# A pre-norm attention and expert block: the order of the next operations searched in a queue model while the program is built, projections of all batches in one row

## The chip, the cores and the metric

One core of a Trainium2 chip. A core has TensorE (PE, matrix products into PSUM), VectorE (DVE), ScalarE (ACT), GpSimd (POOL) and SyncE (SP), which issues the transfers between main memory and on-chip memory. PSUM has 8 banks of 128 x 512 fp32. Each engine works through its own queue in order. The metric is device time in microseconds of one launch.

## The reference

x is 4 x 2048 x 256 (four batches, 8192 rows); 16 heads of 16 channels; 8 experts, of which each row takes 2.

```
x = x + attn(layernorm(x))
    attn(x): q, k, v = x @ w_qkv.T + b_qkv
             softmax(q k^T / 16) v per head, @ w_o.T + b_o + x
x = x + ffn(layernorm(x))
    ffn(x): scores = softmax(x @ w_gate.T); the best 2 of 4 groups by the sum of (score + bias), then the best 2 experts
            h = silu(xe @ w1[e]) * (xe @ w3[e]); routed = h @ w2[e]
            out = silu(x @ sw1.T) * (x @ sw3.T) @ sw2.T, and routed rows added to the rows that flat_idx names
```

`flat_idx` holds expert numbers 0 to 7, so that the routed part lands in the first 8 rows of the output only.

## The kernel before, in words

**Attention.** Work is cut into 64 units (batch, group of 4 heads, chunk of 512 queries). For the last batch the units are ordered in two halves of chunks, so that its first chunks end early. A unit has 64 products M (tile mx: 128 queries x 512 keys, with 63 rows contracted), each read by one DVE maximum into ms; the maxima are transposed (mt), negated (mr) and written by a small DMA as row 63 of the unit's queries qst; then 64 products S (tile st: 128 keys x 512 queries), each read by one ACT exponential into et; and 16 steps A (tile av: four matmuls of 128 keys in four column groups), each of which needs four exponentials. At a unit's end ACT copies av to ao and a DMA stores it in ad. M of a unit must be complete before its first S; M runs ahead of S by LEAD (line 32) key tiles beyond a unit. M and S contract 64 rows, alternate between the halves of the array (last digit of the tile's name), and a pair in the two halves runs together.

**Projections and posts.** Each batch has four chunks of projections (`qkv`, line 423: layer norm, transposes pt_x, four qk_proj with tile pp, two v_proj with tile pv, which go to the DRAM tensors kd, qd, vd) and four chunks of posts (`post`, line 845: `heads_in` reads ad and divides by the softmax sums, po is the output projection, then layer norm, transposes, routing (`route`, lgT), and the shared expert pa, pb, pd). `tables` (line 516) multiplies expert weights for the routed part (tile ta). All of these are Python generators that yield what they need next; `step` runs one piece. kd, qd, vd, ad are two DRAM buffers each, used by batch modulo 2; rows 48 to 63 of kd and 16-row padding of qd are written once per buffer from `pad` by `fill_rows` (line 303).

**The order.** PE, DVE, POOL and ACT instructions stand in the order in which the Python program issues them; SP's queue is ordered by the framework. `Plan` (line 36) keeps a clock per engine while the program is built; it decides which pieces are ready, and `mtile` (line 211) takes, of seven banks for M, S and all projections, the one that the plan says is free first. The loop at the end of `body` (line 1345) walks a fixed string:

```
PATTERN = "SADSMMSMDSSPDMMMMSSSASMMSSMAMSSMMSAMMMSS"
```

`token` (line 1303) runs M, S or A, for P a projection block (`do_p`) if its rate says that one is owed, for D a piece of DVE work (`do_d`). The rate spreads what is queued over the batch. `enter` (line 1168) queues, at the first unit of batch b, the projections of batch b+1, the posts of batch b-1 and, in the last batch, the tables. `loads` (line 1186) issues the loads of unit u+2 in unit u, once the projections of its batch are done. When the last A is issued the loop ends; what is left of side jobs, posts and projections is issued after it (`while side or posts or queue`), then the last heads, and `finish` with the last two chunks' shared expert and the routed part (mo, mu, pg).

All instructions go through the wrapper at line 48, so the profile names them L48: they are told apart by tile names, from which numbers of buffers and units are left out.

Of the kernel before, what the change touches and what calls it, by code (L numbers as in the profile page):

```python
# [2 lines left out]

# [25 lines left out]
BIG = 3e38  # L29
LEAD0 = 3  # L30
LEAD = 6
NET = 6
BANKS = 7


class Plan:
# [109 lines left out]

    def book_sp(self, name, out, ins, k):
        self.run("SP", out, ins, 60, self.waits(out, ins, 100), 2300 + out.size() / 40)


def const_array(rows):
# [32 lines left out]
def body(tc, B, L, cols, x, wqkv, bqk, wst, bst, bv, wo, bo, wg, w1, w2, w3, sw1, sw2, sw3, ebias, cst, pad, out):  # L184
# [107 lines left out]

    kst = [cp.tile([P, 2, L], F32R, tag=f"kst{i}", name=f"kst{i}") for i in range(2)]
    qst = [cp.tile([P, 2, QC], F32R, tag=f"qst{i}", name=f"qst{i}") for i in range(3)]
    kd = [dr.tile([H, 64, L], F32, tag=f"kd{i}", name=f"kd{i}") for i in range(2)]
    qd = [dr.tile([H, 64, L], F32, tag=f"qd{i}", name=f"qd{i}") for i in range(2)]
    vd = [dr.tile([P, 4, NK, VW], F32, tag=f"vd{i}", name=f"vd{i}") for i in range(2)]
    ad = [dr.tile([H, 32, L], F32, tag=f"ad{i}", name=f"ad{i}") for i in range(2)]
    resd = dr.tile([B * L, D], F32, tag="resd", name="resd")

    nhalf = cp.tile([P, TQ], F32, tag="nhalf", name="nhalf")
# [56 lines left out]
    def qk_proj(b, c, m, alloc=None):  # L358
        n = f"{b}_{c}_{m}"
        xT = xTs[b, c]  # L360
        w = w_k if m >= 2 else w_q
        tok = slice(c * QC, (c + 1) * QC)
        msl = slice((m % 2) * P, (m % 2 + 1) * P)
        if alloc:
            pp = alloc(f"pp_{n}")
            mm3(pp, w, xT, msl, slice(0, QC))
            yield
        else:
            pp = stile(f"pp_{n}")
            yield from mm3g(pp, w, xT, msl, slice(0, QC))  # L370
        hi = sb.tile([P, QC], F32R, tag="hi", name=f"hi_{n}", bufs=3)
        lo = sb.tile([P, QC], F32R, tag="lo", name=f"lo_{n}", bufs=3)
        f = sb.tile([P, QC], F32, tag="qkf", name=f"qkf_{n}", bufs=2)
        S.activation(f, pp, AF.Identity, bias=b_qk[:, m:m + 1])
        if alloc:
            S.copy(hi, f)
        else:
            S.activation(hi, pp, AF.Identity, bias=b_qk[:, m:m + 1])
        mark["G"] = G.tensor_tensor(lo, f, hi.bitcast(F32), ALU.subtract).ins
        h0 = 8 * (m % 2)  # L380
        dst = (kd if m >= 2 else qd)[b % 2]
        for r, src in enumerate((hi, hi, lo) if m >= 2 else (hi, lo, hi)):
            Q.dma_start(dst[h0:h0 + 8, 16 * r:16 * r + 16, tok], src.bitcast(F32))

    def v_proj(b, c, half, alloc=None):
        n = f"{b}_{c}_{half}"
        xT = xTs[b, c]
        vt = vts[half]
        pv = alloc(f"pv_{n}") if alloc else stile(f"pv_{n}")
        for j in range(2):  # L390
            i = 2 * half + j
            mm3(pv[:, j * D:(j + 1) * D], xT, w_v, slice(i * P, (i + 1) * P), slice(0, D))
            if not alloc and j == 0:
                yield need("c2", 705)
        if alloc:
            yield
        for j in range(2):
            S.copy(vt[:, :, j, 0:68].rearrange("p g (h c) -> p g h c", c=17)[:, :, :, 0:16],
                   pv[:, j * D:(j + 1) * D].rearrange("p (g h c) -> p g h c", g=4, c=16))
        k0 = c * TQ + 2 * half  # L400
        Q.dma_start(vd[b % 2][:, :, k0:k0 + 2, :], vt)

    xls = {}

# [266 lines left out]
    def heads_in(b, c, nh, aT, ahl):  # L671
# [2 lines left out]
        w = H * QC // P  # L674
        s1 = sb.tile([P, w], F32, tag="s1", name=f"s1_{n}", bufs=1)[0:nh * QC // w, :]
        tok = slice(c * QC, (c + 1) * QC)
        Q.dma_start(s1, ad[b % 2][0:nh, 16, tok].rearrange("h (a n) -> h a n", n=w))
        parts = [(t, min(P, 16 * nh - P * t)) for t in range(2) if 16 * nh > P * t]
        for t, np_ in parts:
            Q.dma_start(aT[0:np_, t, :], ad[b % 2][8 * t:8 * t + np_ // 16, 0:16, tok])  # L680
        yield need("d", 480, s1)
        V.reciprocal(s1, s1)
        rd = dr.tile([H * QC], F32, tag="rd", name=f"rd_{n}", bufs=2)
# [198 lines left out]


    queue, posts, side = deque(), deque(), deque()
    todo = [8, 0]
    first_need = need("p")
    wants = {}
# [9 lines left out]

    def load_unit(u):
        b, g, c = units[u]
        for t, src, new in ((qst[u % 3], qd[b % 2][4 * g:4 * g + 4, :, c * QC:(c + 1) * QC], True),  # L900
                            (kst[int(kset[u] % 2)], kd[b % 2][4 * g:4 * g + 4], fresh[u])):
            if new:
                Q.dma_start(t.bitcast(F32), src.rearrange("(p h) r n -> (h r) p n", p=2))

    def load_v(u):
        b, g, c = units[u]
        if fresh[u]:
            vst[kset[u]] = sb.tile([P, NK, VW], F32, tag="vst", name=f"vst_{kset[u]}", bufs=2)
            mark["D"] = Q.dma_start(vst[kset[u]], vd[b % 2][:, g]).ins

    urgent = deque()
    turned = set()
# [42 lines left out]
    def finish_unit(u, av):  # L955
# [4 lines left out]
        def out_():  # L960
            ao = sb.tile([P, QC], F32, tag="ao", name=f"ao_{u}", bufs=1)
            S.copy(ao, av)
            Q.dma_start(ad[b % 2][4 * g:4 * g + 4, :, c * QC:(c + 1) * QC].rearrange("h r n -> (h r) n"), ao)
            if b == B - 1 and g == 3:
                posts.append(post(b, c))
                todo[1] += 12
            if u == len(units) - 2:
                posts.append(post_first(B - 1, NPER - 1))

        urgent.append((need("a", 470, av), out_))  # L970


    ps_p = tc.tile_pool(name="ps_p", bufs=4, space=PSUM)
# [166 lines left out]
    def setup():  # L1140
# [8 lines left out]
            W[n] = split(n, t, eng=G)  # L1149
        with tc.issue_after(mark["D"]):  # L1150
            fill_rows(kd[0], 0, 0, 4)
        for h in (0, 8):
            yield from fill(1, h, h + 8)

    w_g = cp.tile([P, 2, 32], F32, tag="w_g", name="w_g")
    e_b = cp.tile([P, E], F32, tag="e_b", name="e_b")
# [11 lines left out]
    def enter(u):  # L1168

        b, g, c = units[u]  # L1170
        if u == 1:
            posts.append(setup())
        if u % (4 * NPER) == 0:
            for w in range(NPER):
                if b + 1 < B:
                    nqkv[b + 1] = qkv(b + 1, w)
                    queue.append(nqkv[b + 1])
                    todo[0] += 8
                if b:
                    posts.append(post(b - 1, w))  # L1180
                    todo[1] += 12
            if b == B - 1:
                posts.append(tables())
                todo[1] += 9

    def loads():

        u, kt = ns // (4 * NK), ns // 4 % NK
        if u + 2 < len(units) and u + 2 not in loaded and kt >= 4:
            b, g, _ = units[u + 2]  # L1190
            if (nqkv[b] if b else others if g > 1 else None) not in queue:
                load_unit(u + 2)
                loaded.add(u + 2)
        if kt >= NK // 2 and u + 1 < len(units) and u + 1 not in valued:
            load_v(u + 1)
            valued.add(u + 1)
# [6 lines left out]
    def do_s():  # L1203
# [8 lines left out]
            es[ns // 2] = plan.opened("e", NET, sb.tile([P, 2, QC], F32, tag="et", name=f"et_{u}_{kt}_{p}", bufs=NET))  # L1212
        et = es[ns // 2]
        S.activation(et[:, j, :], st, AF.Exp, scale=SCALE)
        ns += 1

    def do_a():
# [8 lines left out]
        for t in e2:  # L1226
            et_free[t.tensor.name] = plan.drained
        na += 1
        if kt == NK - 1:
            finish_unit(u, av)  # L1230

# [11 lines left out]
    def heads():  # L1243

        for n, fn in list(urgent)[:1]:
            yield n, (lambda fn=fn: (urgent.popleft(), fn()))
        for jobs in (side, posts, queue) if todo[1] > todo[0] else (side, queue, posts):
            if jobs:
                yield wants.get(id(jobs[0]), first_need), (lambda jobs=jobs: step(jobs))

# [30 lines left out]
    def do_p():  # L1281

        nonlocal owed
        x = heavy("ms", 150)
        if not x:
            return
        x[1]()
# [2 lines left out]
            lights()  # L1290
            heavy("c", INF)[1]()

    def do_d(most):
        nonlocal credit
        credit = min(1500.0, credit + most)
        while True:
            x = heavy("d")
            if not x or x[0][1] > credit + 300:
                return
            x[1]()  # L1300
            credit -= x[0][1]

    def token(k):
        nonlocal held, owed
        if k == "M":
            if nm < NM and nm // (NK * MXS) in loaded and nm / MXS < ns / 4 + NK + LEAD + 2:
                do_m()
        elif k == "S":
            u = ns // (4 * NK)
            if ns < 4 * NS and ns - 4 * na < 2 * NET:  # L1310
                while u not in turned:
                    if nm < (u + 1) * NK * MXS:
                        do_m()
                    else:
                        urgent_now()
                do_s()
        elif k == "A":
            if held > 0:
                held -= 1
            elif na < NS and 4 * na + 4 <= ns:  # L1320
                do_a()
        elif k == "P":
            left = 4 * NPER * NK - na % (4 * NPER * NK)
            owed = min(3.0, owed + RATE * (sum(todo) + left // NK) / max(8, left // 4 - SPARE))
            for _ in range(2):
                if owed >= 0.5:
                    lights()
                    do_p()
        elif k == "D":
            do_d(450)  # L1330

    def urgent_now():
        while urgent:
            urgent.popleft()[1]()

    PATTERN, LAG, RATE, SPARE = "SADSMMSMDSSPDMMMMSSSASMMSSMAMSSMMSAMMMSS", 2, 1.0, 6
    owed, held, credit = 0.0, LAG, 0.0
    others = rest()
    queue.append(others)
    for h in (4, 8):  # L1340
        for _ in fill(0, h, 2 * h):
            pass
    plan.level()
    with tc.manual_schedule(engines={ENG.PE, ENG.DVE, ENG.Pool}):
        tick = 0
        while na < NS:
            loads()
            lights()
            if nm < NM and nm // (NK * MXS) not in loaded and nm / MXS < ns / 4 + NK + 1:
# [6 lines left out]
                elif light()[1] < INF:  # L1356
                    plan.clock["PE"] = max(plan.clock["PE"], light()[1])
                continue
            token(PATTERN[tick % len(PATTERN)])
            if tick % 8 == 4 and nm / MXS < ns / 4 + NK + LEAD:  # L1360
                token("M")
            tick += 1
        while urgent:
            urgent.popleft()[1]()
    ordered.__exit__(None, None, None)
# [67 lines left out]
```

## Time and profile before

| | |
|---|---|
| median of 3 runs (lowest, highest) | 3239.95 us (3238.51, 3249.52) |
| profiled execution, its own time | 3235.01 us |
| its span, first to last instruction | 3232.6 us |
| mean granted clock of PE | 0.971 |
| busy: PE, weight loads, DVE, ACT, POOL | 3070.5, 1399.5, 2816.2, 2532.3, 540.1 us |
| transfers | 233.81 MB, mean 72 GB/s |

The page's second part shows the same over 40 slices of 81 us (digits are tenths of the slice):

```profile
PE   7899999999999999999999999999999999999968
DVE  7799989998899998997899999999789899899456
ACT  5688878887878788888688888888687777777834
PEclk9899999999999999999999999999999999999978
```

and its fifth part the groups of instructions (engine, operation, out<-in, shapes, count, then busy us, mean ns of one, and the engine's idle time before them):

```profile
L48 DVE TENSOR_REDUCE ms<-mx 128x1 f32<-128x512 f32 x4096 | 2526.4, 682 | 238.8 <-PE mx L48 194.7
L48 ACT ACTIVATE et<-st 128x512 f32<-128x512 f32 x4096 | 2153.6, 604 | 497.3 <-PE st L48 377.5
L48 PE MATMUL st<-qst,kst 64*128 64x512 f32 x4096 | 1245.6, 439 | 62.4 <-DMA qst<-mr 26.2
L48 PE MATMUL mx<-kst,qst 63*128 63x512 f32 x4048 | 1197.3, 452 | 20.6 <-DVE ms L48 8.3
L48 PE MATMUL av<-et,vst 128*32 128x512 f32 x8192 | 1116.3, 617 | 16.4 <-ACT ao L48 16.1
```

Successive instructions of an engine overlap, so the mean of one is longer than the distance from one to the next; a step A appears as eight matmuls.

### The profile page before, as it was taken

Reading aid. Unit: us, or ns where it says so; the run is one execution under the profiler, and the core shown is the slowest. Engines: PE = TensorE matmul, PEld = TensorE weight load, DVE = VectorE, ACT = ScalarE, POOL = GpSimd, SP = SyncE. Lnnn points to the kernel's source line nnn. Section 1 sums busy time; section 2 is a strip of 40 time slices with the busy share of each in tenths; the row PEclk is TensorE's granted clock in tenths of the full one; section 3 lists DMA queues with packets and bytes.
Section 4 is the critical chain, followed back from the end, with each engine's and each line's share of the span. In section 5 each row is a group of like instructions: output and inputs, shape, how many; then the busy total and the mean of one; then the engine's idle time right before and its main releaser. Section 6 shows DMA issues by size and latency. Waiting matters only on the chain. (4 is left out here: it accounts for less than half of the span.)

```text
span 3232.6 us, 52783 instructions
## 1 busy us (share of the span) xinstructions
PE 3070.5 (95%) x19507; PEld 1399.5 (43%) x19507; DVE 2816.2 (87%) x5053; ACT 2532.3 (78%) x4979; POOL 540.1 (17%) x498
## 2 busy tenths in 40 slices
PE   7899999999999999999999999999999999999968
PEld 5434444443444444444344444444344344444346
DVE  7799989998899998997899999999789899899456
ACT  5688878887878788888688888888687777777834
POOL 5101011010112112211111112121011111110143
PEclk9899999999999999999999999999999999999978
DMA  5543131131212122222112122222112111212010
GB/s 155 181 144 100 49 105 50 44 104 33 79 46 98 48 87 67 80 82 67 59 37 93 56 64 93 74 69 65 58 47 76 62 66 68 75 34 79 25 47 27
DMA packets 135677, 233.81 MB, mean 72 GB/s; under 512 B 13179, under 2 KB 70651, under 8 KB 130427
## 3 DMA queue, kind: packets, MB, share of 16 engines
q1 hardware_dynamic: 135419, 230.44, 21.6%
q8 instruction: 153, 2.51, 0.3%
q14 instruction: 105, 0.86, 0.1%
HBM read 134.87 MB, written 103.41 MB: 74 GB/s over the span
## 5 line engine op out<-in xcount | busy, mean ns | idle before, releaser
L48 DVE TENSOR_REDUCE ms<-mx 128x1 f32<-128x512 f32 x4096 | 2526.4, 682 | 238.8 <-PE mx L48 194.7
L48 ACT ACTIVATE et<-st 128x512 f32<-128x512 f32 x4096 | 2153.6, 604 | 497.3 <-PE st L48 377.5
L48 PE MATMUL st<-qst,kst 64*128 64x512 f32 x4096 | 1245.6, 439 | 62.4 <-DMA qst<-mr 26.2
L48 PE MATMUL mx<-kst,qst 63*128 63x512 f32 x4048 | 1197.3, 452 | 20.6 <-DVE ms L48 8.3
L48 PE MATMUL av<-et,vst 128*32 128x512 f32 x8192 | 1116.3, 617 | 16.4 <-ACT ao L48 16.1
L48 PEld LDWEIGHTS st<-qst,kst 64*128 64x128 f32 x4096 | 610.0, 188 | 670.1 <-DVE ms L48 412.2
L48 PEld LDWEIGHTS mx<-kst,qst 63*128 63x128 f32 x4048 | 559.1, 188 | 603.8 <-DVE ms L48 352.8
L48 PEld LDWEIGHTS av<-et,vst 128*32 128x32 f32 x8192 | 162.9, 108 | 348.1 <-issue 308.7
L48 POOL TENSOR_TENSOR lo<-qkf,hi 128x512 fp32r<-128x512 f32 x64 | 81.9, 1282 | 590.9 <-ACT hi L48 439.9
L48 POOL TENSOR_TENSOR rs_a<-rs_a,nhalf 128x4 f32<-128x4 f32 x16 | 16.3, 1019 | 424.1 <-DVE rs_a L48 404.5
L48 POOL TENSOR_TENSOR aT<-aT,rb 128x512 f32<-128x512 f32 x30 | 38.7, 1293 | 274.8 <-DMA rb<-rd 273.4
L48 POOL TENSOR_TENSOR th<-th,cs 128x512 f32<-128x512 f32 x30 | 31.2, 1041 | 302.6 <-ACT th L48 302.6
L48 POOL TENSOR_TENSOR hT<-hT,th 128x512 f32<-128x512 f32 x30 | 38.9, 1297 | 251.2 <-ACT hT L48 113.2
L48 DVE TENSOR_TENSOR x<-pd,x 128x512 f32<-128x512 f32 x32 | 22.1, 690 | 64.1 <-PE pd L48 64.1
L48 ACT ACTIVATE qkf<-pp,b_qk 128x512 f32<-128x512 f32 x64 | 44.3, 692 | 36.7 <-PE pp L48 36.5
L48 POOL TENSOR_TENSOR rs_b<-rs_b,nhalf 128x4 f32<-128x4 f32 x16 | 16.2, 1015 | 284.6 <-DVE rs_b L48 264.1
L48 ACT ACTIVATE x<-x,rs_b 128x256 f32<-128x256 f32 x64 | 33.1, 589 | 18.2 <-DVE rs_b L48 18.2
L48 POOL TENSOR_TENSOR x<-x,xl 128x256 f32<-128x256 f32 x64 | 46.5, 757 | 0.0
L48 DVE TENSOR_TENSOR x<-po,res 128x512 f32<-128x512 f32 x32 | 22.1, 691 | 27.3 <-PE po L48 27.3
L48 POOL TENSOR_TENSOR x<-x,b_o 128x256 f32<-128x256 f32 x64 | 45.4, 743 | 0.0
L48 ACT ACTIVATE xl<-x,rs_a 128x256 f32<-128x256 f32 x64 | 33.2, 590 | 10.3 <-DVE rs_a L48 10.3
L48 ACT COPY ao<-av 128x512 f32<-128x512 f32 x63 | 38.9, 617 | 0.2 <-PE av L48 0.2
(397 smaller groups left out, 2190.8 us busy)
## 6 DMA issues: line engine op xcount, KB each, us to landing
kst<-kd SPq DMA_DIRECT2D x19, 2048.0 KB
qst<-qd SPq DMA_DIRECT2D x63, 512.0 KB
qd<-hi SPq DMA_DIRECT2D x64, 256.0 KB
kd<-hi SPq DMA_DIRECT2D x64, 256.0 KB
ad<-ao SPq DMA_DIRECT2D x63, 256.0 KB
vst<-vd SPq DMA_DIRECT2D x20, 664.0 KB
vd<-vt SPq DMA_DIRECT2D x32, 332.0 KB
x<-x SPq DMA_DIRECT2D x16, 512.0 KB
```

The source lines that it names most:

```text
L48: r = f(*a, **k)
```

## The change

The fixed string, `token` and `do_d` go. A class `Ahead` holds a queue model of PE, DVE and ACT with seven banks, the exponentials' buffers and the accumulator, in nanoseconds. Each turn of the loop fills a window of 46 letters (M, S, A, O for the copy of av, P, D), orders it so that it can run, searches it with 1600 random moves or swaps that are accepted by cost and a falling temperature, and issues the first 10. The window is then filled again. The projections of batches 1 to 3 are all queued at the start, and `rate` spreads projections and posts over all units, with a due time of 2.5 units before a batch begins; a batch's post is queued when the chunk's last group of heads ends. The DRAM tensors kd, qd, vd, ad become four each, and `setup` fills the padding of batches 1 to 3 at once. `loads` takes the next unit when it is closer than two units, too.

```diff
+HORIZON = 46
+COMMIT = 10
+TURNS = 1600
...
+class Ahead:
...
+    def run(self, seq, i, state):
+        (pe, g0, g1, drained, f0, f1, mode, dve, act, ban, exps, free, nm, ns, na, no, vfree, ip, idd) = state
...
+        for c in seq[i:] if i else seq:
+            if c == "M" or c == "S":
...
+                w = ban[0] + 55
+                slow = 0
+                if w > x - 100:
+                    slow = 100
+                    if w > x:
+                        x = w
...
+                pe = x + 4
+                x += 395 + slow
...
+                if c == "M":
+                    x += 40
+                    if x > dve:
+                        dve = x
+                    dve += 598
+                    heapreplace(ban, dve + 85)
+                    nm += 1
+                else:
...
+                    act += 468
+                    heapreplace(ban, act + 105)
+                    exps.append(act + 160)
+                    ns += 1
+            elif c == "A":
+                if len(exps) < 4 or (na % 16 == 0 and no < na // 16):
+                    return None
...
+                pe = g0 = g1 = x + 907
...
+        cost = max(pe, dve - 1500, act - 1500)
+        return cost + 0.3 * (max(pe - dve, 0) + max(pe - act, 0))
...
+    def search(self, seq, state, turns):
...
+        for _ in range(turns):
+            new = seq[:]
+            a = int(rnd() * n)
+            b = int(rnd() * n) if rnd() < 0.5 else a + int(rnd() * 13) - 6
...
+            if rnd() < 0.5:
+                new.insert(b, new.pop(a))
+            else:
+                new[a], new[b] = new[b], new[a]
...
+            cost = self.run(new[i * step:], 0, marks[i])
+            temp *= 1 - 4.0 / turns
+            if cost is None or (cost > now and rnd() > exp((now - cost) / temp)):
+                continue
...
+        return best
...
-    kd = [dr.tile([H, 64, L], F32, tag=f"kd{i}", name=f"kd{i}") for i in range(2)]
+    kd = [dr.tile([H, 64, L], F32, tag=f"kd{i}", name=f"kd{i}") for i in range(B)]
...
-            if b == B - 1 and g == 3:
+            if g == 3:
                 posts.append(post(b, c))
                 todo[1] += 12
+                posted.append((b, c))
...
-        urgent.append((need("a", 470, av), out_))
+        copies.append(out_)
...
-        for h in (0, 8):
-            yield from fill(1, h, h + 8)
+        for i in range(1, B):
+            for h in (0, 8):
+                yield from fill(i, h, h + 8)
...
-        if u % (4 * NPER) == 0:
-            for w in range(NPER):
-                if b + 1 < B:
-                    nqkv[b + 1] = qkv(b + 1, w)
-                    queue.append(nqkv[b + 1])
-                    todo[0] += 8
-                if b:
-                    posts.append(post(b - 1, w))
-                    todo[1] += 12
-            if b == B - 1:
-                posts.append(tables())
-                todo[1] += 9
+        if u == 4 * NPER * (B - 1) + 1:
+            posts.append(tables())
+            todo[1] += 9
...
+    def rate():
+        done = made / NK
+        r = (sum(todo) + 12 * max(0, nchunk - 2 - len(posted)) + len(units) - done) / max(0.5, len(units) - SPARE - done)
+        return max(r / NK, due())
+
+    def due():
+        done = made / NK
+        return max([(todo[0] - 32 * (B - 1 - b) + 16 * b - SOON - done) / max(1.0, 16 * b - SOON - done)
+                    for b in range(1, B) if nqkv[b] in queue], default=0.0) / NK
...
+    LAG, SOON, SPARE = 2, 2.5, 1.5
...
+    for b in range(1, B):
+        for w in range(NPER):
+            nqkv[b] = qkv(b, w)
+            queue.append(nqkv[b])
+            todo[0] += 8
...
-            token(PATTERN[tick % len(PATTERN)])
-            if tick % 8 == 4 and nm / MXS < ns / 4 + NK + LEAD:
-                token("M")
-            tick += 1
+            state = refill()
+            window, rest_ = search.ordered(window, state)
...
+            window = search.search(window, state, TURNS)
+            for c in window[:COMMIT]:
+                if c == "M" and (nm >= NM or nm // (NK * MXS) not in loaded):
+                    continue
+                give(c)
+                lights()
+            window = window[COMMIT:] + rest_
```

`present` reads the model's start from the plan's clocks, and the next blocks and DVE pieces from the heads of the queues; `refill` tops the window up to 46 letters, four S, up to five M and one A at a time (an O after a unit's last A), puts a P in for each block that the rate says is owed, and a D for each ready piece of DVE work; `give` issues one letter.

## The prediction

> **What bounds the kernel now.** I cut the span at four events (first S 96 us, last row-maximum 3027, last A 3081, end) and read the busy time of each stretch; then, inside the long stretch, the waits; then the places where PE or DVE stood longest; then SP's queue there; then the tail.
>
> Stretches (columns: from:to, length, busy us and instructions of PE, weight loads, DVE, ACT, POOL, then granted clock, DMA share, GB/s):
>
> ```profile
> 0.00:96.00 96.00, 73.34 (x321) 52.39 (x323) 71.65 (x136) 50.04 (x94) 49.80 (x59) 0.96 0.53 166
> 96.00:3027.00 2931.00, 2836.60 (x18091) 1244.26 (x18088) 2640.83 (x4697) 2375.24 (x4651) 415.93 (x378) 0.98 0.22 72
> 3027.00:3081.00 54.00, 52.82 (x334) 19.85 (x330) 9.27 (x32) 49.79 (x100) 13.52 (x10) 1.00 0.11 38
> 3081.00:3232.60 151.60, 107.77 (x769) 83.03 (x767) 94.41 (x189) 57.19 (x136) 60.88 (x53) 0.79 0.12 37
> ```
>
> Call them start, main, close, tail: 96 + 2931 + 54 + 151.6 = 3232.6. In main no engine is full: DVE 90%, ACT 81%, and PE's 97% needs a second look. The skill's rule ("Perfetto Trace Analysis", Identifying the Most-Contended Engine) says that matmul busy time is no measure of PE's headroom and that the weight-load share is; that is 1244/2931 = 42%. By PE's busy row a new order could give 3%; by the rule, PE would be half free. I take neither, but add PE's work up from starts in the timeline:
>
> ```profile
> 1095.88 0.18 PEld L48 LDWEIGHTS mx<-kst,qst 63*128 63x128 f32 x1 [0.84 <-ACT et L48]
> ...
> 1096.82 1.07 PE L48 MATMUL av<-et,vst 128*32 128x512 f32 x8
> 1097.82 0.29 PEld L48 LDWEIGHTS mx<-kst,qst 63*128 63x128 f32 x3 [0.84 <-DVE ms L48]
> ...
> 1098.72 1.06 PE L48 MATMUL av<-et,vst 128*32 128x512 f32 x8
> ```
>
> An A holds PE 1.00 us (1096.82 to 1097.82); six S and M, three in each half of the array, 0.90 (to 1098.72): 0.235 a pair plus 0.19 for the turn. Six 512-column matmuls of a projection start to start take 1.5. Over main's built order that is 999 A x 0.907 = 906, pairs 998, turns 360, projections and transposes 303: PE sums to 2567 us, 88%. DVE: long runs of row-maxima stand 0.598 apart (12.65 us for 21), so 4020 of them are 2410, plus 180 of layer norms, additions and routing: 2590, 88%. Two engines are equally loaded, and each waits for the other through seven PSUM banks.
>
> How coarse that coupling is: I cut main at every A and add up, per piece, the longest of the PE, DVE and ACT sums (ACT 0.48 per exponential). One-A pieces give 2861, two-A pieces 2805, four-A pieces 2724. Main took 2931, of which some 40 are the stops below; 2891 is the one-A sum and 1%. So today hardly anything is evened out between one A and the next. **This is what a better order can win.**
>
> The stops:
>
> ```profile
> 776.64 0.38 SPq L48 DMA_DIRECT2D qst<-qd  x1
> 777.70 1.33 SPq L48 DMA_DIRECT2D qst<-mr  x2
> ```
> ```profile
> 780.37 0.47 PE L48 MATMUL st<-qst,kst 64*128 64x512 f32 x1 [3.55 <-DMA qst<-mr]
> 1578.67 0.76 PE L48 MATMUL st<-qst,kst 64*128 64x512 f32 x1 [4.01 <-DMA qst<-mr]
> ```
> ```profile
> 1519.36 0.69 DVE L48 TENSOR_TENSOR x<-pd,x 128x512 f32<-128x512 f32 x1 [10.80 <-PE pd L48]
> ```
>
> Six times the first S of a unit waits for its row of negated maxima, because on SP a load of qst that must wait for the unit before to end stands ahead of it; DVE then idles 5.0 to 5.6. Twice (ends of batches 1 and 2) DVE idles 10.8 + 2.1: 24 S run without an M, as the next batch's queries are not projected yet.
>
> **The change, part by part.**
>
> *Searched order.* Counts in main stay (4,019 M, 1,006 A). Turns hardly change (q stretches 1,242 to 1,283 over the loop; A still come singly but for six pairs). What changes is the mix: 3 M or 7 M per A before, 1 to 8 after, and M and S take turns. The same ledger on the new order: one-A pieces 2830, two-A 2728, four-A 2680. Lower end for main without stops: the four-A sum, if seven banks even out that far; upper end: the one-A sum plus the same 1%, 2858. The planner's prices agree with rows (M 598 ns against 0.598, A 907 plus a drain against 1.00, exponential 468 against 0.478 at best), so I take the nearer row for a planned order: two-A plus 1%, **2755**. Against it: 327 A now stand at most four S behind the ones they need (before: two), so a late exponential reaches PE.
>
> *Projections in one row.* The 24-S droughts at units 30 and 46 are gone from the order; they are in the ledger already. The counterpart is that loads no longer alias two DRAM buffers; DRAM waits were not on any path.
>
> *SP's queue.* Every load and row write counts: in the built order six qst loads again stand ahead of a row write they should follow (units 2, 3, 11, 24, 41, 58 for 8, 14, 15, 16, 32, 48). No gain, 32 + 8 stay.
>
> *Padding of four buffers.* New: eight writes of 16 rows x 8 heads x 2048 x 4 B = 1.05 MB, in one block with the two that existed, ahead of unit 3's query load. Before, the last of those is issued at 162.5 and that load at 163.3. 8.4 MB at 261 to 322 GB/s (100:110 and 190:200 of the windows) is 26 to 32 us that SP's queue is late. Unit 3's first M is the 192nd, 116 after the 76 of the start, at 0.73 each: about 181. The load lands near 197, PE stands with S and A queued behind that M. Range 0 (there is slack I can't see) to 35 (the row of unit 2, behind a 2 MB key load, is later still); I take **18**. Main: 2755 + 40 + 18 = 2813, or 118 less.
>
> *Close.* Before, 91 S, 25 A and four projection blocks followed the last M. After, 64 S and 18 A and no block, but the last four M stand behind 14 S, so the row of the last unit is not ready: 0.2 for the last maximum, 0.9 transpose, copy and hand-overs, 2.7 from the row's issue to the S (777.70 to 780.37 above), then 64 exponentials x 0.534 = 34.2 (the 8.62 us of sixteen at 3026.13) and the last A with its copy, 3: **41**, 13 less.
>
> *Tail.* The cost that the edit does not show. The loop ends before its posts are done: by the built order, 96 pd, 48 pa, 48 pb, 72 po beyond (3,2) and (3,3), and all 32 table matmuls follow the last A, where before 24, 12, 12 and 18 and no table did. That is chunk (2,2) from its transposes, (2,3), (3,0), (3,1), one behind the other. Before's tail shows one chunk alone:
>
> ```profile
> 3078.95 0.39 PE L48 MATMUL po<-w_oh,at_1h 128*128 128x256 f32 x1
> ...
> 3087.87 2.16 PE L48 MATMUL pt_x<-cs,x 128*128 128x128 f32 x8 [4.01 <-ACT x L48]
> ...
> 3113.07 0.39 PE L48 MATMUL po<-w_oh,at_2h 128*128 128x256 f32 x1 [0.59 <-ACT at_2h L48]
> ```
>
> 34.1 us from one po to the next, 25.2 from the transposes. After: 25.2 + 3 x 34.1 = 127.5, and 7 for the tables (eight weight loads over two buffers that the tanh tiles share; 0 to 20). Before, 31.6 lay behind the last A. So **+103**, tail 254. Inside the loop a chunk is 12.9 us of PE. The clock rule ("TensorE: Matmul & The Clock Gate", HAM oscillation) speaks against the move too: PE's idle gaps beyond some 3.4 us halve the clock. Here the gap before pd was 5.6 and pd matmuls then stand 0.21 apart, against 0.12 for po at full clock; the tail's clock is 0.79. At full clock 24 of them would take 2.8 instead of 5.1, a chunk some 31; the row, slow clock included, is what I use.
>
> **Sum.** 96 + 2813 + 41 + 254 = 3204 span, 28 below 3232.6. The profiled execution took 3235.0, 2.4 more than its span, and lies 5 below the median of 3240: 3207 against it, **3212** on the median's scale, 0.9% faster. A measurement of this kernel can tell 0.5% from nothing.
>
> **Rivals.**
> 1. *The leftover chunks decide: slower.* The order stays close to the one-A row: 2858 + 58 = 2916, sum 3307, 3315 on the median's scale; with half the gain, 3264. The point is main's saving: tail and close cost 103 - 13 = 90, so main, padding included, must fall below 2841. For it: the new order still has 697 q stretches of six, like 706 before, and PE and DVE at 88% each leave little. Against: planner prices match the rows. Chance 0.38, about 3270.
> 2. *The two cancel*: main, padding included, saves 74 to 106: 3224 to 3256. Chance 0.16.
> 3. *The banks even out four A's, the padding is hidden*: 2680 + 27 + 40 = 2747, sum 3138 + 8 = 3146. For it: lead of M over S is steady at 84 to 94, so the search can shift work. Against: one bank holds one tile, and S, M and projections share seven. Chance 0.13.
> 4. *The order does nothing because DMA paces main*: its share there is 0.22; dropped.
>
> **How the numbers follow.** Forecast 3165 to 3224, 0.33; rival 3, 0.13; cancelling 0.16; rival 1, 0.38. Faster 0.46, same 0.16, slower 0.38. The range reaches from rival 3 almost to rival 1's upper sum, **3146 to 3310**, and leaves about 0.07 and 0.1 outside; the forecast's own is 3165 to 3224.
>
> **What would show it.** Main from first S to last row-maximum near 2813, with DVE idle down from 290 to about 200 and no 10.8 us gap; a stop of PE near 180 to 200 us with DMA above 0.8; about 41 us from the last maximum to the last A; a tail near 254 with four po blocks 34 apart and the clock below 0.8. Wrong if main saves less than 90 with the padding, if chunks in the tail overlap (tail under 220), or if PE waits for et before av by more than a few tens of us.

## The result: a little slower, and the profile after

| | before | after |
|---|---|---|
| median (lowest to highest), 5 runs each | 3239.7 us (3238.5 to 3249.5) | 3263.5 us (3260.1 to 3267.7) |
| ratio, 95% interval | | 1.0070 [1.0051, 1.0089] |
| span of the profiled execution | 3232.6 us | 3258.3 us |
| mean granted clock of PE | 0.971 | 0.960 |

The time was forecast at 3212 us, faster; it is 24 us (0.7%) slower than before. The slices of 81 us:

```profile
PE   7849999999999999999999998999999999998668
DVE  7748999898999989999999998989999998993456
PEclk9879999999999999999999999999999999999678
```

Three things stand out against before. The third slice of PE and of DVE has a hole (4). The middle of DVE's row has more nines. The last four slices thin out, and the clock with them (6, 7, 8), where before only two did. The same in the windows of the trace, cut at the same four events (columns as in the prediction):

```profile
0.00:96.00 96.00, 73.33 (x320) 51.94 (x322) 72.30 (x137) 49.81 (x93) 49.80 (x59) 0.96 0.52 163
96.00:2958.80 2862.80, 2767.15 (x17875) 1195.20 (x17873) 2608.99 (x4611) 2338.15 (x4609) 375.73 (x343) 0.98 0.22 74
2958.80:2998.50 39.70, 36.85 (x214) 11.87 (x215) 2.71 (x10) 34.26 (x70) 1.02 (x1) 0.91 0.08 24
2998.50:3258.30 259.80, 182.06 (x1101) 143.64 (x1101) 144.63 (x296) 87.44 (x207) 115.56 (x95) 0.73 0.16 50
```

Main fell by 68, close by 14, tail rose by 108: together the 26 us of the spans. The counts matter: main has 86 DVE instructions fewer than before (4,611 for 4,697), the tail 107 more. Work was moved out of main, so part of the 68 is no better order at all.

The groups of instructions, with DVE's and PE's idle time before them:

```profile
L54 DVE TENSOR_REDUCE ms<-mx 128x1 f32<-128x512 f32 x4096 | 2525.7, 680 | 246.3 <-PE mx L54 186.3
L54 PE MATMUL mx<-kst,qst 63*128 63x512 f32 x4048 | 1252.5, 445 | 58.5 <-DMA qst<-qd 40.5
L54 PE MATMUL st<-qst,kst 64*128 64x512 f32 x4096 | 1249.4, 442 | 33.8 <-DMA qst<-mr 19.7
```

A new wait of M for a load of queries, 40.5 us, has come; the wait of S for its row has fallen from 26.2 to 19.7. In the timeline the 40.5 is a single stop, and SP's queue ahead of it shows why:

```profile
224.73 0.76 PE L54 MATMUL mx<-kst,qst 63*128 63x512 f32 x1 [40.53 <-DMA qst<-qd]
```
```profile
170.79 0.63 SPq L54 DMA_DIRECT2D qd<-pad  x1
175.37 0.63 SPq L54 DMA_DIRECT2D kd<-pad  x1
180.19 0.63 SPq L54 DMA_DIRECT2D qd<-pad  x1
185.06 5.40 SPq L54 DMA_DIRECT2D kd<-hi  x2
194.74 0.58 SPq L54 DMA_DIRECT2D kd<-lo  x1
199.57 0.37 SPq L54 DMA_DIRECT2D qst<-qd  x1
```

Before, the same load was issued at

```profile
163.31 0.51 SPq L48 DMA_DIRECT2D qst<-qd  x1
```

The padding's first writes, up to the one at 170.79, are issued 0.67 us apart, the later ones 4.6 to 4.9. A write is 1.05 MB, and 1.05 MB in 4.8 us is 219 GB/s; all transfers between 170 and 200 us moved 212 GB/s. So the queue seems to take a new write only as fast as an old one is done. Unit 3's load is issued at 199.57, 36 us later than before, and it is there only 25 us after that, when M starts.

For what follows I divide main again, in all kernels alike: *stops*, which are the idle gaps of DVE of 3 us or more in the timeline, and *order*, which is the rest. Before: 57 and 2874. After: 86 (40.2 of them the stop at 225 us) and 2776.

### The profile page after: what moved, and what is told of

The parts are those of the page before. It is cut to its first block, busy times and chain, and to the rows that moved or that the text cites. A ratio compares the mean times of both kernels' runs of the same rounds, so it can differ in the third digit from the quotient of the medians.

```text
span 3258.3 us, 52647 instructions
## 1 busy us (share of the span) xinstructions
PE 3059.4 (94%) x19507; PEld 1402.7 (43%) x19507; DVE 2828.6 (87%) x5053; ACT 2509.7 (77%) x4979; POOL 542.1 (17%) x498
## 5 line engine op out<-in xcount | busy, mean ns | idle before, releaser
L54 PE MATMUL mx<-kst,qst 63*128 63x512 f32 x4048 | 1252.5, 445 | 58.5 <-DMA qst<-qd 40.5
L54 PE MATMUL st<-qst,kst 64*128 64x512 f32 x4096 | 1249.4, 442 | 33.8 <-DMA qst<-mr 19.7
L54 PE MATMUL av<-et,vst 128*32 128x512 f32 x8192 | 1103.7, 609 | 7.2 <-ACT et L54 6.7
L54 PEld LDWEIGHTS mx<-kst,qst 63*128 63x128 f32 x4048 | 589.2, 186 | 625.5 <-DVE ms L54 274.1
L54 PEld LDWEIGHTS st<-qst,kst 64*128 64x128 f32 x4096 | 592.6, 186 | 617.5 <-DVE ms L54 304.9
L54 ACT ACTIVATE hi<-pp,b_qk 128x512 fp32r<-128x512 f32 x56 | 38.2, 682 | 4.2 <-DMA qd<-hi 4.2
```

The source lines that it names most:

```text
L54: r = f(*a, **k)
```

## The experiments

All ratios stand against the kernel before on the same chip, where its median was 3248 to 3249 us. When the changed kernel was measured it was 3240 us, so single times and parts compare across kernels only to some 10 us. "M", "S", "A", "P" and "D" are the letters of the window, and a chunk has 24 pd matmuls.

**The padding alone, taken out of the change and put into the kernel before.** e1:

```diff
-        for i in range(1, B):
-            for h in (0, 8):
-                yield from fill(i, h, h + 8)
+        for h in (0, 8):
+            yield from fill(1, h, h + 8)
...
             posts.append(setup())
+        if u in (4, 6, 8, 10):
+            posts.append(fill(2 + (u > 6), 8 * (u // 2 % 2), 8 * (u // 2 % 2) + 8))
```

> The searched kernel, with the padding of batches 2 and 3 written in four lots of two at units 4, 6, 8 and 10 instead of eight writes in one block at unit 1. Theory P (the block holds up unit 3's query load): the one stop of PE of 40.5 us near 184 to 225 us goes, the first 300 us of main lose about 40, time near 3263 - 40 = 3223; the tail stays near 260. Rival: the load is late for another reason (the 0.5 MB loads of x around it, or the projections it reads), the stop stays above 20 us and the time at 3250 or more.

Measured 3222.7 us, ratio 0.9916 [0.9891, 0.9940]: theory P. e3 is the kernel before with four DRAM buffers of each kind and all of `fill(1..3)` in `setup`:

> The kernel before with four DRAM buffers of each kind and the padding of all of them in one block, its order untouched. Theory P: a stop of about 40 us at unit 3's first M, time 3240 + 40 = 3280. The prediction's size: 18, so 3258. Rival (the stop needs the new order's other loads): below 3245.

Measured 3282.3, ratio 1.0102 [1.0079, 1.0125], with a stop of 37.0 us of M for qst<-qd at 216: theory P again, in the old order. And e6, with batch 2's padding at the start and batch 3's in two lots later:

> The changed kernel with the padding of batch 2 still at the start, that of batch 3 in two lots at units 8 and 10: four extra writes in the block instead of eight. Theory (each of the writes holds up unit 3's query load by its own transfer): the stop of 40.5 us shrinks by four times 4.8 us, the distance between SP's issues there, to 21; time about 3243. Rival A (the stop begins only past some depth of the queue): under 8 us, about 3225. Rival B (it is the wait of that load behind others, not the padding's amount): over 33, about 3257.

Measured 3246.6 in a single execution, so without an interval. M in the pages of e1, e6 and e3:

```profile
L54 PE MATMUL mx<-kst,qst 63*128 63x512 f32 x4048 | 1255.3, 446 | 20.0 <-ACT et L54 6.8
L54 PE MATMUL mx<-kst,qst 63*128 63x512 f32 x4048 | 1255.1, 445 | 38.4 <-DMA qst<-qd 20.8
L48 PE MATMUL mx<-kst,qst 63*128 63x512 f32 x4048 | 1202.1, 453 | 56.8 <-DMA qst<-qd 37.0
```

So 0, 4 and 8 extra writes (e1, e6, after) give stops of 0, 20.8 and 40.5 us on PE: 5 us for each 1.05 MB, and no slack shows. The order part is 2776 in after, 2777 in e1 and 2780 in e6, so the padding touches little else.

**No search** (e2):

```diff
-TURNS = 1600
+TURNS = 0
```

> The searched kernel with no search turns: the window is issued as it is filled and made runnable (S, M, A in turn, a P at place 12, a D at place 4). Theory L (the search pushes P and D letters behind the ten that are issued, and so leaves four chunks and the tables behind the last A): by the built order nothing is left behind but the last two chunks, the tail falls from 260 to about 120. Theory O (the search packs main better): main rises from 2862 to 2960 or more, as M, S and A in plain order leave the banks empty or full. Both together: near 3230. Rival to O (the search packs nothing): main within 40 of 2862 plus 40 for the chunks that come into it, and a time near 3165.

Measured 3418.1, ratio 1.0516 [1.0494, 1.0538]. Theory L's tail came (114), and main rose by 296 us, where theory O said 100 or more. The refill's order without moves is far worse than the string of before: its order part is 3104, 230 above before's. Page of e2, the groups of row-maxima and of M:

```profile
L54 DVE TENSOR_REDUCE ms<-mx 128x1 f32<-128x512 f32 x4096 | 2539.2, 681 | 399.8 <-PE mx L54 372.8
L54 PE MATMUL mx<-kst,qst 63*128 63x512 f32 x4048 | 1158.1, 449 | 98.3 <-DVE ms L54 57.9
```

DVE waits for PE 373 us where in after it waits 186, and M waits for banks that DVE still reads (57.9 us): each waits for the other. To learn whether the runs of four S and five M were to blame, I laid both down in turns, with no search and the padding spread (e7), and then two and two (e9; the diff is e7's):

```diff
-            more += ["M"] * max(0, min(want, 5))
+            m = max(0, min(want, 5))
+            more = [c for k in range(5) for c in "MS" if k < (m if c == "M" else len(more))]
```

> No search (TURNS = 0), but the refill lays M and S down in turns (M S M S ... A) instead of four S, then up to five M, then A; padding spread as in e1. In e2 the unsearched order stood 125 us above the sum over one-A pieces, where before, after and e4 stood within 70 below to 13 above it. Theory (runs of one kind use up the banks, and PE, DVE and ACT take turns in standing still): alternation alone brings main back to about the order before: total 3150 to 3210. Rival (it is the search over all letters that packs; alternation is not enough): e2 less the padding's 40, 3340 or more; in between, both.

> As e7, no search and the padding spread, but the refill lays M and S down two and two (M M S S ... A). M and S of the same number use the same half of the array, so e7's single turns put 3858 M and S right behind one of the same half, which alone is 190 us by 0.235 each; two and two put 23 so. Theory (the mix decides, e7 failed for the halves alone): 3160 to 3230. Rival (a fixed mix, with P and D put in between, isn't enough; the search finds where each P, D and M goes): e2 less the padding's 40: 3330 to 3390.

Measured 3416.3 and 3390.9, ratios 1.0519 [1.0494, 1.0545] and 1.0450 [1.0423, 1.0477]: the rival's numbers, twice, but not its reason. How M and S are mixed is not what counts, and the ledger does not see the loss: its one-A sums of 2984, 3002 and 2989 for e2, e7 and e9 lie within 2% of the 2946 of the searched e5 below. M and S of the same half behind one another, which I priced at 190 us, cost at most the 26 us between e7's main and e9's; in the trace PE starts both as two M, two S, two M, two S.

What the three unsearched orders have in common is the place of A. All three refills lay four S and mostly four M between one A and the next. Cut PE's row from the first S to the last M into runs of M and S that nothing else interrupts. The runs sum to 1757 us in e9 and 1786 in e7 against 1502 in e5, for 8,018 to 8,048 products; all else on PE adds up to 1371 to 1386. In e9 717 of the runs have eight products and take 1.71 us (median); in e5 670 have six and take 0.91, and its 48 runs of eight take 1.70. Here is one of eight in e9 (PE's rows, and of the weight loads, PEld, the last) and one of six in e5:

```profile
1504.70 0.50 PE L54 MATMUL mx<-kst,qst 63*128 63x512 f32 x2
1505.04 0.40 PE L54 MATMUL st<-qst,kst 64*128 64x512 f32 x2
1505.28 0.40 PE L54 MATMUL mx<-kst,qst 63*128 63x512 f32 x2
1505.52 0.96 PE L54 MATMUL st<-qst,kst 64*128 64x512 f32 x2
1505.98 0.18 PEld L54 LDWEIGHTS st<-qst,kst 64*128 64x128 f32 x1 [0.51 <-DVE ms L54]
1506.40 1.07 PE L54 MATMUL av<-et,vst 128*32 128x512 f32 x8
```
```profile
1508.19 0.50 PE L54 MATMUL mx<-kst,qst 63*128 63x512 f32 x2
1508.52 0.40 PE L54 MATMUL st<-qst,kst 64*128 64x512 f32 x2
1508.77 0.40 PE L54 MATMUL mx<-kst,qst 63*128 63x512 f32 x1
1508.77 0.39 PE L54 MATMUL st<-qst,kst 64*128 64x512 f32 x1
1509.09 1.07 PE L54 MATMUL av<-et,vst 128*32 128x512 f32 x8
```

The eighth product's weights wait 0.51 us for DVE to finish a maximum. Seven banks serve M, S and projections, so waiting for a bank is the likely reading. The fixed string of before has 705 runs of six and 430 of seven, and at like work its order part lies within some 20 to 30 us of the searched ones (worked out below), not 235 to 273 above. So most of the packing does not take a search. That the length of the runs is the cause rests on these traces; no run changes it alone.

**Pieces P and D kept where the refill puts them** (e4; the search moves M, S, A and O only):

```diff
-            if not 0 <= b < n or new[a] == new[b]:
+            if not 0 <= b < n or new[a] == new[b] or new[a] in "PD" or new[b] in "PD":
```

> The searched kernel in which the search may not move the letters P and D, so that they come up when they were put in; all else as it is, padding in one block. Theory L: nothing but the last two chunks is left behind the last A, tail near 120 instead of 260; main takes three and a half chunks and the tables back, 13 us of PE each: 2862 + 45 to 60 = 2910 to 2920; time near 3175 (3150 to 3200). Rival: what the search wins it wins by choosing where projection blocks stand; then main goes to 2980 or more and the time to 3240 or more.

Measured 3177.0, ratio 0.9776 [0.9753, 0.9798]: theory L. By the built order 48 pd are left behind the last A instead of 144, and no table; the tail is 114. The padding is still paid, in another place. Its block is issued behind the load of queries this time, the last write at 197.7, but ahead of a row of unit 2, on which an S waits until 34 us after the row's issue:

```profile
202.77 5.72 SPq L54 DMA_DIRECT2D qst<-mr  x2
```
```profile
237.24 0.76 PE L54 MATMUL st<-qst,kst 64*128 64x512 f32 x1 [29.80 <-DMA qst<-mr]
```

**Both repairs together** (e5: e4's edit and e1's), and **only D fixed** (e8: e1's edit, and the search may move P):

> P and D pieces keep the places of the refill (as in e4) and the padding of batches 2 and 3 is written in four lots between units 4 and 10 (as in e1). In e4 the eight writes still cost a stop, only in another place: the first S of unit 2 waited 29.8 us for its row. Theory (leftover and padding are two prices that add): that stop goes, e4's 3177 less some 30: 3139 to 3155, with a tail of 114 as in e4. Rival (the writes must be paid somewhere; four at a time they stand before a row write or a load that PE needs): 3170 or more.

> Padding spread; only D is kept where the refill puts it, P may be moved. By the built order 36 more pd and 36 more po stay behind the last A than in e5. Theory (the price is the number of chunks left, each some 36 us in the tail and some 19 to 20 inside main): 20 to 30 above e5, tail 160 to 175. Rival (what moving P wins in main pays for the chunks left): equal to e5 or below.

e5 took 3139.9, ratio 0.9671 [0.9642, 0.9699]: **3.3% faster than before**, the best of all. e8 took 3185.3, ratio 0.9808 [0.9784, 0.9832]. The windows of e5 and of e8, main and tail:

```profile
96.00:2984.70 2888.70, 2847.72 (x18301) 1247.93 (x18298) 2660.18 (x4763) 2383.05 (x4701) 444.60 (x397) 0.99 0.23 77
3024.30:3137.80 113.50, 84.03 (x669) 65.45 (x664) 72.37 (x145) 47.12 (x117) 42.32 (x38) 0.85 0.10 31
```
```profile
96.00:2984.80 2888.80, 2822.62 (x18178) 1228.52 (x18178) 2646.96 (x4723) 2369.88 (x4680) 424.52 (x384) 0.99 0.23 76
3026.30:3183.00 156.70, 111.41 (x793) 86.12 (x785) 95.20 (x190) 58.29 (x138) 63.05 (x54) 0.79 0.12 39
```

Main is equally long in both, though e8 has 40 DVE instructions fewer in it; they reappear in a tail longer by 43. So e8 is 45 above e5, more than the 20 to 30 expected: of what the lighter main saves (order 2846 for 2869), stops take back all (43 for 20, among them eleven waits for a row, 25.9 us).

**P and D laid down earlier** (e10: e5 with places 4 + 8 p and 2 + 6 d):

> e5 with P laid down at places 4 + 8 p of the window instead of 12 + 16 p, and D at 2 + 6 d instead of 4 + 12 d. By the built order only one po block fewer is left behind the last A, the other leftovers are equal. Theory (what is left sets the tail, and main holds the same work): within 12 of e5's 3140, tail 110 to 114. Rival (pieces issued sooner than their inputs make DVE and PE wait in order): 3155 or more, with stops of DVE behind transfers or projections.

Measured 3159.8, ratio 0.9739 [0.9712, 0.9767]. A miss for both: the tail is 109, near what was expected, but main is some 20 us longer than e5's, and not by stops (16 us): the order itself packs worse. It has 557 runs of six where e5 has 670.

The parts of all kernels (us; the start is 96 in each; leftover is pd matmuls behind the last A in the built order):

| | order | stops | close | tail | span | leftover |
|---|---|---|---|---|---|---|
| before | 2874 | 57 | 54 | 152 | 3233 | 72 |
| after | 2776 | 86 | 40 | 260 | 3258 | 144 |
| e1 padding spread | 2777 | 50 | 41 | 259 | 3222 | 144 |
| e6 half of the padding early | 2780 | 69 | 41 | 259 | 3245 | 144 |
| e3 before with padding | 2882 | 94 | 54 | 152 | 3277 | 72 |
| e2 no search | 3104 | 54 | 46 | 114 | 3413 | 48 |
| e7 in turns, no search | 3142 | 16 | 47 | 114 | 3415 | 48 |
| e9 in pairs, no search | 3121 | 11 | 46 | 115 | 3389 | 48 |
| e4 P, D fixed | 2871 | 58 | 40 | 114 | 3179 | 48 |
| e8 D fixed, spread | 2846 | 43 | 42 | 157 | 3183 | 84 |
| e5 P, D fixed, spread | 2869 | 20 | 40 | 114 | 3138 | 48 |
| e10 the same, earlier | 2893 | 16 | 41 | 109 | 3154 | 48 |

e3 has the same M, S and projections between its A as before, and e6 the same as after; their orders differ by 9 and 4 us all the same. Differences of that size in this column say nothing. Of e2's stops, 43 us are one wait of DVE for a load of x near 231; with the padding spread (e7) that wait is 5.

## Why the forecast went to the wrong side

Against the sum of 3204 for the span, 3258.3 came: 54 more. Two terms of the sum failed, both in main: the padding was taken at 18 us and cost 40, and the searched order was taken at 2755 and took 2776. These 43 us alone turn the 28 forecast as a gain into a loss. By steps:

- **Padding, "I take 18": wrong, 40.2.** +22. M was due at 181 and stopped at 184. The landing of the load was forecast near 197, which is about when it was issued (199.6): I took the issue for the landing, which came 25 us later, and then let "there is slack I can't see" stand for a reason. e6 and e1 show none. The rate was too high as well: 261 to 322 GB/s, read in two stretches of the kernel before, where the block ran at some 212 to 219. It came out even above the range's 35.
- **Searched order, "two-A plus 1%, 2755": 2776.** +21. It lies midway between the new order's one-A and two-A sums (2830 and 2728): by that measure the search evens out less than two A's. And of the gain of 98 against before's 2874, about half or more is not packing: the forecast said that the counts stay, and looked at M and A only, while three chunks of posts and the tables had left main, which the ledger booked as gain. What they are worth there can be estimated from e5 against e8 and e1, all with the padding spread: order falls by 23 for 36 pd (1.5 chunks) and by 92 for 96 pd (4 chunks and tables), 15 to 23 a chunk, where the forecast spoke of 12.9. (The letters that the search may move differ between these runs too, so the price holds both.) Three chunks are 45 to 69 of the 98. e8, with nearly before's leftover (84 pd for 72), is 28 below before in order and 40 in order and close together, half a chunk included: at like work its search packs some 20 to 30 us better than the string.
- **Stops, "32 + 8 stay": 46 without the padding.** +6, but by other causes than forecast. The two droughts of 10.8 are gone, as said, and S's waits for rows fell over the whole span from 26.2 to 19.7. New ones came, the largest a wait of 9.5 for M at 1965, and this one:

```profile
743.96 0.55 DVE L54 RECIPROCAL s<-s 128x64 f32<-128x64 f32 x1 [7.89 <-DMA s<-ad]
```

  Here DVE stands in order behind a transfer for a post. That wait for s in main is 7.9 to 8.5 us in after, e1 and e6, where D may move, and nowhere over 2 in e4, e5, e8 and e10, where it may not.
- **Close, 41: right, 39.7.**
- **Tail, 254: right, 259.8.** The first po of the leftover chunks, one of each:

```profile
3020.86 0.39 PE L54 MATMUL po<-w_oh,at_3h 128*128 128x256 f32 x1 [0.55 <-ACT at_3h L54]
...
3056.93 0.39 PE L54 MATMUL po<-w_oh,at_0h 128*128 128x256 f32 x1 [0.32 <-ACT bT L54]
...
3095.04 0.58 PE L54 MATMUL pd<-s_2h,hT_0h 128*128 128x256 f32 x1 [10.28 <-ACT hT_0h L54]
...
3102.66 0.38 PE L54 MATMUL po<-w_oh,at_1h 128*128 128x256 f32 x1 [0.55 <-ACT at_1h L54]
...
3137.03 0.38 PE L54 MATMUL po<-w_oh,at_2h 128*128 128x256 f32 x1 [0.55 <-ACT at_2h L54]
```

  They stand 36.1, 45.7 and 34.4 apart (forecast 34.1, and 7 for the tables); the longest holds a wait of 10.28 for ACT. The clock of the tail fell from 0.79 to 0.73, the direction in which the rule on the clock gate that the prediction cites pointed. The price of a chunk was read from a row at the slow clock, so most of it was in the sum already.
- **Late exponentials before A** (tens of us, if wrong): 6.7 us in all. Didn't come.

Sum: 22 + 21 + 6 - 1 + 6 = 54. **Rival 1's outcome is what happened**, and its point held: tail and close cost 94 (forecast 90), main had to fall below 2841, and it was 2863. Its premise did not hold: the order did not stay at the one-A row of 2858 but fell to 2776, and the padding took back the difference to its form "with half the gain, 3264". That 3263.5 was measured, so close to it, is luck. With the padding spread main is 2827 and the kernel is faster than before. Repairing the other half, the leftover, pays more: 1.5 chunks cost 43 in the tail, 4 chunks 146, which is 29 to 36 a chunk for 15 to 23 inside. In spans the two repairs give 36 and 80 alone and 121 together, so they add up, nearly.

What e5 wins over before, 95 us of span, comes from order 5, stops 37, close 14 and tail 38. Order and close belong together, since main took in work from both: it has 210 PE instructions more than before, close 113 fewer (221 for 334) and the tail 100 fewer. In the stops the two droughts are gone, and the waits for a row fell from 26.2 to 2.2 us. So "this is what a better order can win", as the forecast put it, named the smaller part: most is in stops and at the end.

Open: why the search puts P and D off past the letters that are issued, beyond the fact that forbidding it brings the leftover from 144 pd to 48; why hardly an S waits for its row in e5; and whether runs of six would pack as well without any search in the new kernel.

## What to carry to other kernels

Before booking a lower sum for a stretch as better packing, count in the built order what has left the stretch, and price it where it went: here a chunk cost some 15 to 23 us inside and 29 to 36 behind the end. A sum of work per piece doesn't see who waits for whose bank inside the piece: look at how long runs of a given length take before trusting it. A scheduler that issues only the head of its window needs a rule against putting off side work. Where a block of large writes is moved ahead of a load, take the whole queue time, landing included, and no discount for slack that no row shows; then spread the block.

## What the hardware showed unexpectedly

- Writes of 1.05 MB each are issued 0.67 us apart at first and then 4.6 to 4.9 (after); each one more ahead of the load made PE stop 5 us longer (0, 20.8, 40.5 for 0, 4, 8).
- The same block, issued after that load instead (e4), stopped an S for 29.8 us at its row of 4 KB: here a small transfer was as late as the large ones ahead of it in the queue.
- Six M and S in a row take 0.91 us (median in e5, in many mixes); eight take 1.67 in e2, 1.71 in e7 and e9.
- In the stop of 40.5 us PE's granted clock fell to 0.50 (after, 200 to 225 us).
- The granted clock of the tail is lower the more leftover chunks it holds: 0.85 at 114 us (e5), 0.79 at 157 (e8), 0.73 at 260 (after).
